# Picked rows in two halves of a PSUM bank, six one-hots under way and a ring of 64 rows: a four-layer graph network on one core

## The chip, the cores and the metric

The kernel runs on one core of a Trainium2 chip. The time is the device time of one execution in microseconds (us), the median of several runs. The engines are TensorE (PE; its weight loads are counted apart as PEld), VectorE (DVE), ScalarE (ACT), GpSimd (POOL) and SyncE (SP). Each engine works through its own list of instructions in order; an instruction that waits holds up everything behind it on that engine.

## The reference, cut to what matters

There are 16 graphs of 1024 nodes with 64 features and a random adjacency of about 16 neighbours a node. Layers 0 and 1 are dense products with the adjacency. Layers 2 and 3 thin out each node's neighbours and aggregate by quantiles: for every node and every feature the values of the node itself and of its remaining neighbours are sorted, and three interpolated quantiles are summed with weights.

```python
# layer 0: tanh(concat(x, adj @ x) @ W1 + b1) @ W2 + b2;   layer 1: (adj / deg) @ x
# layers 2 and 3, each followed by a residual sum and a layer norm:
adj_d = dilate(adj, mask)                # removes every skip-th neighbour, symmetrically
vals  = where((adj_d > 0)[..., None], x[:, None, :, :], big)
sv    = sort(vals, axis=2)               # per node and feature
for tau, wt in zip((0.25, 0.5, 0.75), (0.25, 0.5, 0.25)):
    pos = tau * (m - 1)                  # m: number of values of this node
    agg = agg + wt * (lower + frac * (upper - lower))
y = relu((x + agg) @ W1 + b1) @ W2 + b2
```

## The kernel before

The nodes of a graph are ordered by how many values they have and cut into eight tiles of 128 nodes. Tile t holds up to `SIZES[t]` values a node, and VectorE sorts them with a network of min and max over whole tiles. How a tile's values come into SBUF differs:

- the seven smaller tiles (19, 17, 15, 14, 13, 11 and 10 values, in that order) are gathered by GpSimd from a table in DRAM, one indirect DMA for each value, into a ring of `ROOM` rows. A tile takes adjoining rows of the ring, and its gathers wait until whoever held them has been weighed;
- the largest tile (33 values) is picked by TensorE: for value i VectorE writes a one-hot matrix (`hot`), and 24 matmuls multiply it with the features in three bf16 parts, into PSUM (`pgk`). ScalarE copies the picked rows into `got`.

A "round" k handles layer 2 of graph k together with layer 3 of graph k - 2, so most tiles are sorted as pairs, and there are 18 rounds.

```python
SIZES = (10, 11, 13, 14, 15, 17, 19, 33)
HOTS = 4
ROOM = 72
# ...
def pick(dst, hot, parts, first=True):
    for c in range(NT):
        for q in range(3):
            nc.tensor.matmul(dst, hot[:, c, :], parts[:, c, q, :], start=first and c + q == 0,
                             stop=c == NT - 1 and q == 2)
# ... in fill(k), for the tile of 33 values, for each of the two members:
for g in range(1, size, 8):
    pg = s.psum.tile([P, 8, C], F32, name="pgk", tag="f", bufs=1)      # one PSUM bank
    for i in range(g, g + 8):
        hot = s.lists.tile([P, NT, P], BF, name="hot", bufs=HOTS)
        dve.tensor_scalar(hot, e.place, float(i), None, op0=ALU.is_equal)
        # ... (a first matmul for rows that not all nodes have)
        pick(pg[:, i - g, :], hot, e.parts[m], whole)
        yield 2.1
    yield 2
    nc.scalar.copy(got[:, m, g : g + 8, :], pg)
    yield 0.5
```

The order of every engine's instructions is fixed when the program is built. Each stage is a Python generator; `yield 2.1` says "go on when VectorE has been given 2.1 us more of work", by a rough count of VectorE's work. Between the min and max steps of a sort the kernel lets every generator that is due go on. So `yield` sets a distance in the program, not a wait on the chip.

Three other stages have their distances changed. In `features` (layers 0 and 1):

```python
for h in range(NH):
    pa = s.psum.tile([P, G, C + 1], F32, name="pa", tag="x", bufs=1)
    for q in range(G):
        for jt in range(NT):
            nc.tensor.matmul(pa[:, q, :], adj[i][:, jt, :], x1[:, jt, :], ...)
        yield 4
        # ... near, and the load of the next adjacency block
    yield 6
    dve.tensor_scalar(deg[:, 0], pa[:, :, C], 1.0, None, op0=ALU.max)
```

and earlier in the same stage, two operations on one PSUM tile that the prediction speaks of:

```python
for q in range(G):
    nc.tensor.transpose(px[:C, q * P : (q + 1) * P], x_s[:, h * G + q, :], ident)      # line 427
for q in range(G):
    for jt in range(NT):
        nc.tensor.matmul(px[C:, q * P : (q + 1) * P], x_s[:, jt, :], adj[t][:, jt, :], ...)   # line 431
    if q == 1:
        nc.scalar.copy(node_in[:C], px[:C])                                             # line 434
    yield 5
```

In `lists` (which neighbours remain, and in which order), loops of this form, where TensorE fills one of two PSUM buffers (`pr`, `pv` or `pk`) while ScalarE reads the other:

```python
for t in range(NT + 1):
    if t < NT:
        pr = s.psum.tile([P, N], F32, name="pr", tag="big", bufs=2)
        # ... matmuls into pr
    yield 3
    if t:
        # ... two activations that read prs[t - 1]
    yield 1.2
```

In `ordered`, the stage after it, single products are put at some distance behind what VectorE prepares for them. SBUF is full: a one-hot takes 2 KB of each partition, a row of the ring 512 bytes.

Of the kernel before, what the change touches and what calls it, by code (L numbers as in the profile page):

```python
# [12 lines left out]
F32 = mybir.dt.float32  # L13
F16 = mybir.dt.float16
BF = mybir.dt.bfloat16
# [6 lines left out]
P = 128  # L22
# [4 lines left out]
LEAST = (1,) + SIZES[:-1]  # L27
KS = -(-(max(SIZES[:-1]) - 1) // 8) * 8
KW = max(SIZES)
HOTS = 4  # L30
ROOM = 72
LONG = 40
BIG = 1e30
EPS = 1e-5
# [178 lines left out]
def adj_resnorm_kernel(ctx: ExitStack, tc: tile.TileContext, x, adj_t, nodemask, w01, b01, w02, b02,  # L213
# [189 lines left out]
    def features(b, e):  # L403

        x_s = s.feat.tile([P, NT, C], F32, name="x_s", bufs=1)
        load_x(b, x_s)
        adj = {}

        def load(i):

            if i < 2 * NT:
                adj[i] = s.feat.tile([P, NT, P], F32, name="adj_r", bufs=3)
                cols = slice(i % NT * P, i % NT * P + P)
                nc.sync.dma_start(adj[i], adj_t[entry(b), :, cols].rearrange("o (t p) i -> p (o t) i", p=P))

        load(0)
        load(1)
        x1 = s.feat.tile([P, NT, C + 1], F32, name="x1", bufs=1)
        y = s.work.tile([P, NT, C], F32, name="y_x", bufs=1)
        dve.memset(x1[:, :, C : C + 1], 1.0)  # L420
        yield 8
        for h in range(NH):

            node_in = s.work.tile([P, HALF], F32, name="node_in", bufs=1)
            px = s.psum.tile([P, HALF], F32, name="px", tag="x", bufs=1)
            for q in range(G):
                nc.tensor.transpose(px[:C, q * P : (q + 1) * P], x_s[:, h * G + q, :], ident)
            for q in range(G):
                t = h * G + q
                for jt in range(NT):  # L430
                    nc.tensor.matmul(px[C:, q * P : (q + 1) * P], x_s[:, jt, :], adj[t][:, jt, :], start=jt == 0,  # L431
                                     stop=jt == NT - 1)
                if q == 1:
                    nc.scalar.copy(node_in[:C], px[:C])  # L434
                yield 5
                load(t + 2)
            yield 5
            nc.scalar.copy(node_in[C:], px[C:])
            yield 3
            nc.tensor.matmul(px[:C], w01s, node_in, start=True, stop=True)  # L440
            yield 9
            hid_t = s.work.tile([C, HALF], F32, name="hid_t", tag="node_in", bufs=1)
            nc.scalar.activation(hid_t, px[:C], AF.Tanh, bias=b01c)
            yield 3
            pd = s.psum.tile([P, G, C], F32, name="pd", tag="x", bufs=1)
            for q in range(G):
                nc.tensor.matmul(pd[:, q, :], hid_t[:, q * P : (q + 1) * P], w02s, start=True, stop=False)
                nc.tensor.matmul(pd[:, q, :], ones_row, bias_rows[0], start=False, stop=False)  # L448
                nc.tensor.matmul(pd[:, q, :], ident, x_s[:, h * G + q, :], start=False, stop=True)  # L449
            yield 10  # L450
            nc.scalar.copy(y[:, h * G : (h + 1) * G], pd)
        yield 4
        yield from settle(x1[:, :, :C], y, "x")
        while b and not entries[b - 1].packed:
            yield 2
        near = s.sets.tile([P, NT, N], F16, name="near")
# [3 lines that stand above are left out]
                i = NT + h * G + q  # L460
                t = i - NT
                rows = slice(t * P, (t + 1) * P)
                for jt in range(NT):
                    nc.tensor.matmul(pa[:, q, :], adj[i][:, jt, :], x1[:, jt, :], start=jt == 0, stop=jt == NT - 1)  # L464
# [12 lines left out]
        e.near = near  # L477
        x2 = s.feat.tile([P, NT, C], F32, name="x2", tag="x_s", bufs=1)
        dve.tensor_add(y, y, x1[:, :, :C])
        yield from settle(x2, y, "x")  # L480
        nc.sync.dma_start(table[0][b % 3][:N, :].rearrange("(t p) c -> p t c", p=P), x2)
        while b >= 2 and not entries[b - 2].filled[0]:
            yield 2
        parts = s.feat.tile([P, NT, 3, C], BF, name="x2p")
        yield from split(x2, parts, y)
        e.parts[0] = parts

    def lists(b, e, pace):
# [29 lines left out]
                prs.append(pr)  # L518
                for h in range(NH):
                    cs = range((h + 1) * HALF // P)  # L520
                    for c in cs:
                        nc.tensor.matmul(pr[:, h * HALF : (h + 1) * HALF], near[:, c, t * P : (t + 1) * P],  # L522
                                         steps[:, ONSET + h * HALF - c * P :][:, :HALF], start=c == 0, stop=c == cs[-1])
            yield 3
            if t:
                for i in range(2):
                    junk = s.work.tile([P, N], F16, name="junk", tag="dist", bufs=3)
                    nc.scalar.activation(junk, prs[t - 1], AF.Sign, bias=lim[:, i, t - 1 : t], scale=-1.0,  # L528
                                         accum_out=cut_at[:, i, t - 1 : t])
            yield 1.2  # L530
        yield 5

        mid, off = st[:, 2], st[:, 3]
# [20 lines left out]
        own = s.work.tile([P, NT, 3], F16, name="own", bufs=1)  # L554
        key = s.work.tile([P, 5, NT], F32, name="key_c", bufs=1)
        pvs = []
        for t in range(NT + 1):
            if t < NT:
                rows = slice(t * P, (t + 1) * P)
# [2 lines left out]
                for c in range(NT):  # L562
# [1 line left out]
                    nc.tensor.matmul(pv[:, cols], near[:, c, rows], scaled[:, c, :], start=True, stop=False)  # L564
                    nc.tensor.matmul(pv[:, cols], takes[:, c, rows], minus_n, start=False, stop=False)  # L565
                    nc.tensor.matmul(pv[:, cols], minus_n, takes[:, t, cols], start=False, stop=True)
            yield 2.8
            if t:
                nc.scalar.activation(left(t - 1), pvs[t - 1], AF.Relu)  # L569
# [32 lines left out]
        for t in (*reversed(range(NT)), -1, -2, -3):  # L602
            if t >= 0:
# [30 lines left out]
    def ordered(b, e, order, own):  # L634
# [41 lines left out]
        for g in reversed(range(0, NT, G)):  # L676
# [4 lines left out]
                                     start=c2 == 0, stop=c2 == c)  # L681
            yield 9
            dve.tensor_mul(place[:, g : g + G, :], pp, place[:, g : g + G, :])
        e.place = place

        e.none = s.feat.tile([KW - 1, P], BF, name="none", bufs=5)
        wts = s.feat.tile([P, NT, most_wanted], F32, name="wts", bufs=5)
        for h in range(NH):
# [6 lines left out]
            dve.tensor_scalar(counted, pn[:KW], nth[:KW], None, op0=ALU.is_equal)  # L695
            if h == NH - 1:
                dve.tensor_scalar(e.none, pn[: KW - 1, G - 1, :], nth[: KW - 1], BIG, op0=ALU.is_le, op1=ALU.mult)
            pw = s.psum.tile([P, G, most_wanted], F32, name="pw", tag="s", bufs=1)
            for q in range(G):
                nc.tensor.matmul(pw[:, q, :], counted[:, q, :], weights[:KW, h * G + q, :], start=True, stop=True)  # L700
# [26 lines left out]
    def fill(k):  # L727
# [6 lines left out]
        for m, b, e in members(k):  # L734
            while e.parts[m] is None or e.xs[m] is None or e.place is None or e.none is None:
                yield 1
            nc.scalar.copy(got[:, m, 0, :], e.xs[m][:, t, :])
            for g in range(1, size, 8):
                pg = s.psum.tile([P, 8, C], F32, name="pgk", tag="f", bufs=1)
                for i in range(g, g + 8):  # L740
                    hot = s.lists.tile([P, NT, P], BF, name="hot", bufs=HOTS)
                    dve.tensor_scalar(hot, e.place, float(i), None, op0=ALU.is_equal)
                    whole = i < LEAST[t]
                    if not whole:
                        nc.tensor.matmul(pg[:, i - g, :], e.none,
                                         ident_b[: KW - 1, i - 1 : i].to_broadcast([KW - 1, C]), start=True, stop=False)
                    pick(pg[:, i - g, :], hot, e.parts[m], whole)
                    yield 2.1
                yield 2
                nc.scalar.copy(got[:, m, g : g + 8, :], pg)  # L750
                yield 0.5
            e.filled[m] = True

    def weigh(k, t, got, agg, which):
# [196 lines left out]
    with ExitStack() as main:  # L951
# [309 lines left out]
```

## Time and profile before

| | before |
|---|---|
| time, median of 3 runs | 5402.21 us (5398.02 to 5413.57) |
| span of the profiled execution | 5411.4 us |
| one-hots written by VectorE | 1024, 435 ns each |
| picking matmuls of TensorE | 24576, some 0.2 us each, pipelined |
| copies of picked rows by ScalarE | 128, 584 ns each |
| gathers issued by GpSimd | 2944, 1137 ns each |
| mean granted TensorE clock | 0.753 of full speed |

How to read it: busy time is the time in which an engine executes; the span is shared by all engines. A line of a view of waits says which engine and line waited, for the result of which engine and line, how long in total, how often, and the longest time. A group's line gives its busy time and the mean of one in ns, then the idle time of the engine just ahead of it and what ended it. "issue" is time that no recorded wait explains. The clock is what the throttle granted TensorE, 1.00 being full speed.

### The profile page before, as it was taken

To read this page: it belongs to the slowest core of one execution; us is meant where nothing else is said; L and a number is where in the kernel's file an instruction comes from. 1 tells how busy PE (TensorE), PEld (TensorE's weight loads), DVE (VectorE), ACT (ScalarE), POOL (GpSimd) and SP (SyncE) were. 2 spreads that over 40 slices of the span, in tenths; PEclk is the share of its full clock that TensorE was granted. 3 is DMA by queue.
4 is the path that set the end of the run, shared out by engine and by line. 5 is a ranking of instruction groups with operands and counts; after the bars stand their busy time and mean duration, and the time that the engine had idled before them with its cause. 6 is when DMAs were issued, how large, how long until landed. Compare 5 with 4: busy or idle time off the path is not lost.

```text
span 5411.4 us, 112427 instructions
## 1 busy us (share of the span) xinstructions
PE 3883.9 (72%) x45304; PEld 2975.3 (55%) x45304; DVE 4454.0 (82%) x8819; ACT 2295.4 (42%) x6086; POOL 3677.3 (68%) x3228
## 2 busy tenths in 40 slices
PE   6888877596977959687695968769596876616343
PEld 5656655374755737465573746657374664515332
DVE  2487777989898897878889787887978789979966
ACT  3364453444545363444536344452634445312222
POOL 0335476877777576767768677776867768777562
PEclk7887887696877778686787868678786867756555
DMA  2222222222222211222221122212112211111010
GB/s 82 64 60 55 65 57 50 52 49 59 56 61 48 58 41 45 52 53 59 46 62 42 41 54 56 58 46 58 44 39 58 55 43 23 26 23 26 17 24 10
DMA packets 420187, 259.37 MB, mean 48 GB/s; under 512 B 106165, under 2 KB 368453, under 8 KB 419653
## 3 DMA queue, kind: packets, MB, share of 16 engines
q0 software_dynamic: 102400, 105.06, 10.1%
q1 hardware_dynamic: 317252, 147.02, 9.7%
q8 instruction: 356, 5.83, 0.5%
q14 instruction: 179, 1.46, 0.1%
HBM read 239.27 MB, written 12.58 MB: 47 GB/s over the span
## 4 chain that ended last, share of the span: by engine, by line
DVE 48%; PE 40%; issue 3%; ACT 3%; POOL 3%; DMA 2%; DVEq 0%; POOLq 0%; ACTq 0%
DVE other L207 18%; DVE got_s L207 12%; PE pgk L355 10%; DVE got L207 9%; PE pk L608 8%; PE pa L464 5%; PE px L431 3%; DVE hot L207 2%; POOL got_s L359 2%; DMA got_s<-table,idx 2%; PE ordered_x L355 2%; PE pd L797 1%; PE pd L796 1%; PE pd L449 1%; PE pd L448 1%
## 5 line engine op out<-in xcount | busy, mean ns | idle before, releaser
L359 POOL DMA_INDIRECT got_s<-table,idx x2944 | 3347.8, 1137 | 1487.2 <-issue 662.2
L355 PEld LDWEIGHTS <-hot 128*128 128x128 bf16 x24576 | 949.0, 108 | 595.5 <-DVE hot L207 514.3
L207 DVE TENSOR_SCALAR hot<-place 128x1024 bf16<-128x1024 f16 x1024 | 439.4, 435 | 393.6 <-PE pgk L355 392.8
L355 PE MATMUL pgk<-x3p,hot 128*128 128x64 bf16 x12288 | 563.0, 215 | 251.7 <-DVE hot L207 182.6
L522 PE MATMUL pr<-steps,near 128*128 128x512 bf16 x1536 | 483.5, 486 | 346.1 <-ACT junk L528 190.5
L355 PE MATMUL pgk<-x2p,hot 128*128 128x64 bf16 x12288 | 477.2, 201 | 252.6 <-DVE hot L207 229.3
L762 ACT ACTIVATE got_s<-got_s,wts 128x64 f32<-128x64 f32 x1568 | 399.9, 336 | 384.2 <-DVE got_s L207 383.9
L522 PEld LDWEIGHTS <-near 128*128 128x128 f16 x1536 | 181.2, 119 | 639.0 <-issue 544.9
L207 DVE TENSOR_TENSOR other<-got_s 128x512 f32<-128x512 f32 (+8 forms) x900 | 513.9, 582 | 12.5 <-DMA got_s<-table,idx 0.3
L207 DVE TENSOR_TENSOR got_s<-got_s 128x256 f32<-128x256 f32 (+7 forms) x918 | 491.2, 537 | 19.3
L608 PE MATMUL pk<-near,order 128*128 128x512 f16 x2048 | 478.4, 389 | 0.0
L565 PE MATMUL pv<-minus_n,takes 128*128 128x128 bf16 x1024 | 239.5, 259 | 250.0 <-DVE takes L207 248.9
L207 DVE TENSOR_TENSOR got_s<-other 128x512 f32<-128x512 f32 (+8 forms) x774 | 408.3, 540 | 8.2
L464 PE MATMUL pa<-x,adj_r 128*128 128x65 f32 x2048 | 376.8, 362 | 49.5 <-ACT x L385 26.9
L464 PEld LDWEIGHTS pa<-x,adj_r 128*128 128x128 f32 x2048 | 361.4, 275 | 74.4 <-ACT x L385 27.2
L565 PEld LDWEIGHTS <-takes 128*128 128x128 bf16 x1024 | 118.3, 116 | 422.7 <-DVE takes L207 278.5
L564 PE MATMUL pv<-scaled,near 128*128 128x128 f16 x1024 | 240.9, 260 | 138.1 <-ACT near L569 137.8
L207 DVE TENSOR_TENSOR other<-other 128x128 f32<-128x128 f32 (+13 forms) x558 | 319.1, 572 | 14.8
L608 PEld LDWEIGHTS <-order 128*128 128x128 bf16 x2048 | 196.4, 100 | 230.8 <-issue 24.6
L750 ACT COPY got<-pgk 128x512 f32<-128x512 f32 x128 | 74.7, 584 | 546.6 <-PE pgk L355 546.6
L528 ACT ACTIVATE junk<-pr,nb_st 128x1024 f16<-128x1024 f32 x256 | 282.1, 1108 | 31.6 <-PE pr L522 30.3
L431 PE MATMUL px<-adj_r,x_s 128*64 128x128 f32 x2048 | 263.3, 285 | 8.8 <-ACT node_in L434 7.4
(204 smaller groups left out, 7532.0 us busy)
## 6 DMA issues: line engine op xcount, KB each, us to landing
adj_r<-in_adj_dram SPq DMA_DIRECT2D x256, 512.0 KB
got_s<-table,idx POOLq DMA_INDIRECT x2944
x_s<-in_x_dram SPq DMA_DIRECT2D x16, 256.0 KB
table<-x SPq DMA_DIRECT2D x16, 256.0 KB
x<-table SPq DMA_DIRECT2D x16, 256.0 KB
table<-x3s,rows POOLq DMA_INDIRECT x128
out_dram<-agg,out_rows POOLq DMA_INDIRECT x128
table<-no_row SPq DMA_DIRECT2D x6, 0.2 KB
```

Of the source, the lines that this page charges most:

```text
L207: return call(*args, **kwargs)
L355: nc.tensor.matmul(dst, hot[:, c, :], parts[:, c, q, :], start=first and c + q == 0, stop=c == NT - 1 and q == 2)
L359: nc.gpsimd.indirect_dma_start(out=dst, out_offset=None, in_=tab, in_offset=bass.IndirectOffsetOnAxis(ap=rows, axis=0))
L431: nc.tensor.matmul(px[C:, q * P : (q + 1) * P], x_s[:, jt, :], adj[t][:, jt, :], start=jt == 0, stop=jt == NT - 1)
L464: nc.tensor.matmul(pa[:, q, :], adj[i][:, jt, :], x1[:, jt, :], start=jt == 0, stop=jt == NT - 1)
L522: nc.tensor.matmul(pr[:, h * HALF : (h + 1) * HALF], near[:, c, t * P : (t + 1) * P], steps[:, ONSET + h * HALF - c * P :][:, :HALF], star ...
L528: nc.scalar.activation(junk, prs[t - 1], AF.Sign, bias=lim[:, i, t - 1 : t], scale=-1.0, accum_out=cut_at[:, i, t - 1 : t])
L564: nc.tensor.matmul(pv[:, cols], near[:, c, rows], scaled[:, c, :], start=True, stop=False)
L565: nc.tensor.matmul(pv[:, cols], takes[:, c, rows], minus_n, start=False, stop=False)
L608: nc.tensor.matmul(cols, order[:, c, t * P : (t + 1) * P], left(c, slice(h * G, (h + 1) * G)), start=c == 0, stop=c == NT - 1)
L750: nc.scalar.copy(got[:, m, g : g + 8, :], pg)
L762: nc.scalar.activation(prods[:, m, i, :], got[:, m, slot_id, :], AF.Copy, scale=e.wts[:, t, i : i + 1])
```

## The change

The change has four parts.

1. Up to six one-hots may be under way in place of four. The 4 KB that this takes of each partition comes from the ring, which shrinks from 72 to 64 rows.
2. The picked rows go to two halves of one PSUM bank in turn, four rows each. The copy of a half is placed after the second pick into the other half, so that TensorE need not stop between two groups.
3. In the loops of `lists` the distance between ScalarE's reading and TensorE's next matmuls into the same buffer grows (1.2 to 3, 1 to 2.6, 1.5 to 3), and the distance between TensorE's matmuls and the reading shrinks by as much.
4. A few products are placed later: 3 us before the first `pv`, 8 in place of 6 before `deg`, and 3 us more at two places of `ordered`.

```diff
-HOTS = 4
-ROOM = 72
+HOTS = 6
+ROOM = 64
@@ features, before deg
-            yield 6
+            yield 8
@@ lists, loop of pr
-            yield 3
+            yield 1.2
             if t:
                 # ... two activations that read prs[t - 1]
-            yield 1.2
+            yield 3
@@ lists, before and in the loop of pv
+        yield 3
         for t in range(NT + 1):
             # ... matmuls into pv
-            yield 2.8
+            yield 1.2
             if t:
                 # ... two activations, the first reads pvs[t - 1]
-            yield 1
-        yield 4
+            yield 2.6
+        yield 3
@@ lists, loop of pk
-            yield 4
+            yield 2.5
             # ... copy of pks[done]
-            yield 1.5
+            yield 3
@@ ordered, after place and after counted
+            yield 3
@@ fill
-            for g in range(1, size, 8):
-                pg = s.psum.tile([P, 8, C], F32, name="pgk", tag="f", bufs=1)
-                for i in range(g, g + 8):
-                    # ... hot and pick
-                    yield 2.1
-                yield 2
-                nc.scalar.copy(got[:, m, g : g + 8, :], pg)
-                yield 0.5
+            waiting = None
+            def empty():
+                nc.scalar.copy(got[:, m, waiting[0] : waiting[0] + 4, :], waiting[1])
+            for i in range(1, size):
+                if i % 4 == 1:
+                    first, pg = i, pgs[i // 4 % 2]
+                # ... hot and pick, into pg[:, i - first, :]
+                yield 2.1
+                if i % 4 == 2 and waiting:
+                    empty()
+                if i % 4 == 0:
+                    waiting = first, pg
+            yield 5
+            empty()
+            yield 0.5
@@ before the rounds
+        picked = s.psum.tile([P, 8, C], F32, name="pgk", bufs=1)
+        pgs = [picked[:, :4, :], picked[:, 4:, :]]
```

More of the change, by code (lines that the diff above doesn't have):

```diff
@@ L697, in ordered @@
                 dve.tensor_scalar(e.none, pn[: KW - 1, G - 1, :], nth[: KW - 1], BIG, op0=ALU.is_le, op1=ALU.mult)
+            yield 3
             pw = s.psum.tile([P, G, most_wanted], F32, name="pw", tag="s", bufs=1)
@@ L737, in fill @@
             nc.scalar.copy(got[:, m, 0, :], e.xs[m][:, t, :])
-            for g in range(1, size, 8):
-                pg = s.psum.tile([P, 8, C], F32, name="pgk", tag="f", bufs=1)
-                for i in range(g, g + 8):
[L741 to L747, printed above, removed]
-                    yield 2.1
-                yield 2
-                nc.scalar.copy(got[:, m, g : g + 8, :], pg)
-                yield 0.5
+            waiting = None
[4 more added lines that the diff above has]
+                    first, pg = i, pgs[i // 4 % 2]
+                hot = s.lists.tile([P, NT, P], BF, name="hot", bufs=HOTS)
+                dve.tensor_scalar(hot, e.place, float(i), None, op0=ALU.is_equal)
+                whole = i < LEAST[t]
+                if not whole:
+                    nc.tensor.matmul(pg[:, i - first, :], e.none,
+                                     ident_b[: KW - 1, i - 1 : i].to_broadcast([KW - 1, C]), start=True, stop=False)
+                pick(pg[:, i - first, :], hot, e.parts[m], whole)
+                yield 2.1
[6 more added lines that the diff above has]
+            yield 0.5
             e.filled[m] = True
```

## The prediction, made before the changed kernel was run

> **What bounds the kernel now.** I began with the page's busy times, to see whether one engine is full.
>
> ```profile
> span 5411.4 us, 112427 instructions
> PE 3883.9 (72%) x45304; PEld 2975.3 (55%) x45304; DVE 4454.0 (82%) x8819; ACT 2295.4 (42%) x6086; POOL 3677.3 (68%) x3228
> ```
>
> None is, but VectorE is nearest: 4454.0 us is a floor that the change leaves alone, and 957 us of the span are VectorE's idle time. So the second view is what VectorE waited for, over the whole span:
>
> ```profile
> DVE hot L207 <- PE pgk L355: 392.8, 169, 7.3
> DVE deg L207 <- PE pa L464: 88.6, 20, 6.2
> ```
>
> 393 of the 957 us are VectorE about to write a one-hot while TensorE still reads the one that stood in that buffer four earlier. To see where, I took one round of the steady part. In the chain in order of time the same piece ("DVE other", 4.50 us) returns at 2570.11, 2887.32 and 3204.92, so a round lasts 317 us. Here it is cut into stretches (TensorE, weight loads, VectorE, ScalarE and GpSimd busy; then granted clock, DMA share, GB/s):
>
> ```profile
> 2887.00:2957.00 70.00, 31.85 (x268) 24.27 (x267) 68.50 (x96) 47.29 (x96) 56.92 (x43) 0.72 0.17 43
> 2957.00:2997.00 40.00, 36.48 (x451) 30.22 (x452) 38.42 (x89) 18.58 (x46) 31.77 (x28) 0.72 0.19 37
> 2997.00:3057.00 60.00, 59.26 (x849) 41.77 (x848) 35.63 (x63) 17.09 (x37) 41.35 (x43) 1.00 0.26 60
> 3057.00:3107.00 50.00, 42.61 (x638) 36.45 (x636) 46.58 (x92) 18.24 (x60) 22.14 (x16) 0.79 0.08 17
> 3107.00:3137.00 30.00, 30.00 (x296) 27.36 (x295) 18.50 (x43) 6.56 (x26) 23.30 (x23) 0.50 0.37 95
> 3137.00:3205.00 68.00, 44.03 (x340) 25.87 (x336) 65.38 (x132) 35.44 (x118) 53.37 (x49) 0.75 0.26 62
> ```
>
> Two stretches hold the loss. In 2997 to 3057 TensorE is full (59.26 of 60) and VectorE works 35.63; in 3107 to 3137 TensorE is full and VectorE works 18.50. Elsewhere VectorE is all but full while TensorE idles. So the bound changes inside the round: VectorE, then TensorE, and the four one-hot buffers are all that lets one run ahead of the other. The third view is what TensorE waited for in four rounds (2570 to 3840 us):
>
> ```profile
> PE pv L565 <- DVE takes L207: 71.5, 24, 12.1
> PE pr L522 <- ACT junk L528: 60.4, 12, 8.1
> PE pv L564 <- ACT near L569: 50.2, 16, 9.1
> ...
> PE pgk L355 <- DVE hot L207: 36.3, 26, 4.8
> PE pgk L355 <- ACT got L750: 12.1, 7, 2.7
> ```
>
> The reader should check where these fall: the pr and pv work lies at 2887 to 2950 and 3165 to 3205, where VectorE does not wait for TensorE at all. The fourth view is GpSimd in the same four rounds:
>
> ```profile
> L359 POOL DMA_INDIRECT got_s<-table,idx x737 | 845.0, 1147 | 306.6 <-issue 170.3 <-DVE other L207 81.0 <-DMA got_s<-table,idx 28.3
> L808 POOL DMA_INDIRECT table<-x3s,rows x32 | 46.5, 1453 | 24.0 <-ACT x3s L385 15.5 <-issue 7.0 <-ACT got_s L762 1.2
> L808 POOL DMA_INDIRECT out_dram<-agg,out_rows x32 | 39.1, 1222 | 9.7 <-issue 4.0 <-ACT got L762 3.0 <-DMA got_s<-table,idx 1.5
> ```
>
> A gather costs 1.147 us and about 0.30 us of issue after it. 737 x 1.447 = 1066 us, and the 64 scatters with their gaps some 105 us: 1171 of 1270 us, 92%, or 293 us of each 317 us round. GpSimd looks 68% busy on the page and is in truth the second bound, with about 24 us of slack a round, most of it the 81.0 us of waiting for ring rows.
>
> **What the Trainium skill says.** "TensorE: Matmul & The Clock Gate", part 1 (the HAM clock gate): after an idle window of about 3.4 us TensorE runs at half rate, and sustained work lifts that; the practical advice is to leave no such gaps. The trace agrees only in part: 3107 to 3137 is 30 us of full TensorE at a granted clock of 0.50. Filling gaps is therefore no promise of a faster clock, and I count none. The same page, part 2 (what happens when you issue a matmul), says matmuls stay in program order; the trace agrees, a pv that waits 12.1 us for takes holds everything behind it. "PSUM — Partial Sum Buffer", on bank collisions, says two engines must not touch one bank and the same 32 partitions at once, whatever the columns, and that software must keep them apart. If this program does that by bank, two halves of one bank are no double buffer. The trace has a test, the copy of px into node_in at line 434, whose data the transposes of line 427 wrote:
>
> ```profile
> L427 PE MATMUL px<-ident,x_s x8: 272/349/418, 2940.5 to 3003.6; 128*64 128x128 f32 x8
> ...
> L434 ACT COPY node_in<-px x2: 579/579/579, 2949.9 to 3013.6; 64x512 f32<-64x512 f32 x2
> ...
>   PE px L431: 9.2, 2
> ```
>
> The transposes were over by 3004, the copy began at 3013.6, and ScalarE had stood idle for the matmuls of line 431, which write other partitions of the bank. So waits here go by bank, and I expect the same for the halves.
>
> **The change part by part.**
>
> *Six one-hots.* VectorE may lead by two more. In 2997 to 3057 it made 13 one-hots in 35.63 us of its own work, one per 2.74 us, so two more are worth up to 5.5 us; in 3107 to 3137 nine in 18.50 us, 2.06 us each, up to 4.1 us. That caps the gain at 9.6 of the 31 us that a round loses (125.0 us in four). A longer lead makes the deg wait longer (6.1 us a round, it needs TensorE to have caught up), so I take 6.5 us. Laying the recorded TensorE and VectorE durations end to end with six buffers in place of four gave 6.2 us a round. Over 13 rounds: -85 us.
>
> *TensorE's parts behind what they wait for.* pr waits 60.4/4 = 15.1 us and pv 50.2/4 = 12.6 us a round for ScalarE. With ScalarE placed 3.0 (was 1.2) and 2.6 (was 1.0) ahead of the next matmuls, against two activations of 1.1 to 1.3 us, nearly all of that should go. But it lies where VectorE is full: worth nothing in a steady round, and some 20 us in all in the first rounds, where VectorE idles with it. deg placed 8 instead of 6 after pa: 2 us a round at best, partly eaten by the longer lead; -15 us over the span.
>
> *Two halves.* Copies go from 128 of 584 ns to 256 of about 372 ns (the 128x256 copy of line 451 has that mean): 95 us for 75, on an engine with room. By bank, the third pick of a group waits for the copy of the other half, and that for the second pick: twice as many round trips, and none of the half microsecond that stood behind each copy. Now they cost TensorE 12.1/4 = 3.0 us a round; doubled and shortened by the smaller copy 4.8. So +1.8 us where TensorE is the bound, +25 us over 14 rounds.
>
> *A ring of 64 rows.* Tiles come as 19, 17, 15, 14, 13, 11, 10. 72 rows hold the first four (65), 64 hold three (51). Placing them by hand, a tile now needs the tile four or five before it to be freed; with 64, three, at times four. The timelines give the lead (a tile's sort ends where its first weight begins on ScalarE): in steady rounds gathers end about 100 us before the sort (the 13's ended at 2999.8, its sort began about 3107), and one tile of lead is 24 to 80 us, so most rounds can pay. At the ends they can't: in the last full round the leads of the 13, 11 and 10 are 34, 23 and 14 us, and in the third round the 10's was 49. I charge 20 us there and 40 us over the last four rounds: +60 us.
>
> Sum: -85 - 20 - 15 + 25 + 60 = -35 us, and 5402 - 35 is about 5367.
>
> **The rivals.** (a) GpSimd becomes the bound. For it: 92% full, and a lost tile of lead cannot be made up. Against: waiting VectorE lets TensorE catch up, so the two waits do not add. If each steady round lost 6 us more, the gain would be eaten: about 5450. (b) The halves really are independent, TensorE never waits for a copy, and ScalarE, no longer held, runs weights earlier; then the +25 turns into some -30 and the time is near 5300. The px lines speak against it. (c) The distances straighten TensorE so far that its clock stays up: the clocks of 0.72, 0.79 and 0.50 say that some 73 us of 2957 to 3137 ran at half rate, and a third of them regained would be 10 us a round, 5240. Against it the 30 us at 0.50 with no gap.
>
> **Range and chances.** The ring (20 to 120) and the one-hots (50 to 120) are each uncertain by some 50 us, the rest by 40; together near 90 either way: 5270 to 5470. Faster by over 2% means below 5294, which needs a rival to be right; slower by over 2%, above 5510, needs the ring to bind in every round. 0.2, 0.7, 0.1.
>
> **What would show it.** Right: hot's wait for pgk falls from 393 to about 300 us and is still VectorE's longest; the pr and pv waits for ScalarE fall below a third while the steady round shortens by only 5 to 8 us; TensorE's wait for got doubles from 65 us; VectorE waits for gathers in the third round and the last ones; GpSimd waits longer for ring rows. Wrong: a steady round under 303 us (rival c or b), or gathers heading VectorE's waits in the middle of the span (rival a).

## The result, and the profile after

The changed kernel takes 5379.86 us (median of 4 runs, 5377.75 to 5385.83); the kernel before, run beside it, 5407.51 us. The ratio is 0.9952, with a 95% interval of 0.9933 to 0.9972: a gain of 28 us, or half a per cent. Predicted were 5367 us and a range of 5270 to 5470.

The page of the changed kernel begins:

```profile
span 5376.9 us, 112554 instructions
PE 3746.3 (70%) x45268; PEld 2875.6 (53%) x45304; DVE 4444.1 (83%) x8819; ACT 2296.3 (43%) x6214; POOL 3659.3 (68%) x3228
```

VectorE and ScalarE are as busy as before (4454.0 and 2295.4 us). So the gain has to be looked for in what VectorE waited for. The view of VectorE's waits, changed kernel (waiting engine and line, what it waited for, total us, times, longest us):

```profile
DVE hot L207 <- PE pgk L355: 127.2, 58, 6.9
DVE y_m L207 <- ACT y_m L812: 115.7, 13, 20.3
DVE other L207 <- DMA got_s<-table,idx: 75.5, 10, 19.2
DVE place L207 <- PE pp L681: 75.3, 15, 9.3
DVE near L207 <- DMA adj_r<-in_adj_dram: 65.5, 14, 9.9
```

The one-hot's wait fell from 392.8 to 127.2 us, a fall of 266 us, and deg's, further down in this view, from 88.6 to 19.0. The kernel gained 28. What came in place are the next four lines. VectorE's wait for y_m, which it takes from ScalarE, was this before:

```profile
DVE y_m L207 <- ACT y_m L800: 33.7, 2, 20.3
```

Its wait for gathers (DMA got_s) was 0.3 us before, for place 21.8, for near 17.0.

The same shift shows in ScalarE's own waits. The copy of picked rows waited for picks, first in the kernel before, then in the changed one:

```profile
ACT got L750 <- PE pgk L355: 546.6, 96, 11.3
```

```profile
ACT got L744 <- PE pgk L355: 1175.5, 196, 18.6
```

ScalarE stands twice as long before these copies. Their own work is as predicted, 256 of 369 ns or 94.5 us, in place of 128 of 584 ns or 75 us; the idle time ahead of them was not.

Of TensorE's waits in the changed kernel, those for ScalarE of which the prediction speaks (three longer ones, for hot, takes and nb_st, are left out):

```profile
PE pr L522 <- ACT junk L528: 149.4, 46, 8.8
PE pv L565 <- ACT near L570: 93.8, 30, 7.3
PE pgk L753 <- ACT got L744: 56.2, 81, 3.4
PE pgk L355 <- ACT got L744: 45.5, 48, 3.7
```

pr and pv waited 190.5 and 137.8 us for ScalarE before, so they lost a fifth and a third, not the two thirds hoped for. The wait for the copy went from 69.0 us (65.2 + 3.8) to 101.7.

Last, the crowded part of a steady round of the changed kernel, up to the end of the tile of 33 (two of its stretches; columns as in the prediction: TensorE, weight loads, VectorE, ScalarE, GpSimd, then clock, DMA share, GB/s):

```profile
2982.00:3042.00 60.00, 53.38 (x803) 38.84 (x800) 43.17 (x77) 21.80 (x63) 27.00 (x29) 0.91 0.09 17
3042.00:3082.00 40.00, 31.70 (x465) 27.96 (x464) 30.62 (x68) 8.18 (x33) 31.24 (x26) 0.84 0.28 69
```

Before, TensorE was full in two stretches of the crowded part (59.26 of 60, 30.00 of 30) and busy 42.61 of the 50 us between them. From 2982 to 3082 neither it (85.08 of 100) nor VectorE (73.79 of 100) is full: here they wait for each other and for ScalarE, the idlest of the three (29.98 of 100).

### The profile page after: what moved, and what is told of

It reads as the page before. It is cut to its first block, busy times and chain, and to the rows that moved or that the text cites. A ratio compares the mean times of both kernels' runs of the same rounds, so it can differ in the third digit from the quotient of the medians.

```text
span 5376.9 us, 112554 instructions
## 1 busy us (share of the span) xinstructions
PE 3746.3 (70%) x45268; PEld 2875.6 (53%) x45304; DVE 4444.1 (83%) x8819; ACT 2296.3 (43%) x6214; POOL 3659.3 (68%) x3228
## 5 line engine op out<-in xcount | busy, mean ns | idle before, releaser
L355 PEld LDWEIGHTS <-hot 128*128 128x128 bf16 x24576 | 881.8, 104 | 611.8 <-DVE hot L207 468.2
L522 PE MATMUL pr<-steps,near 128*128 128x512 bf16 x1500 | 435.1, 453 | 378.0 <-ACT nb_st L503 223.8
L355 PE MATMUL pgk<-x3p,hot 128*128 128x64 bf16 x12288 | 493.2, 204 | 229.0 <-DVE hot L207 203.0
L355 PE MATMUL pgk<-x2p,hot 128*128 128x64 bf16 x12288 | 478.6, 201 | 239.1 <-DVE hot L207 216.1
L744 ACT COPY got<-pgk 128x256 f32<-128x256 f32 x256 | 94.5, 369 | 1186.0 <-PE pgk L355 1175.5
L207 DVE TENSOR_SCALAR hot<-place 128x1024 bf16<-128x1024 f16 x1024 | 436.5, 437 | 129.8 <-PE pgk L355 127.2
L207 DVE TENSOR_TENSOR got_s<-got_s 128x384 f32<-128x384 f32 (+7 forms) x918 | 490.7, 537 | 17.5
L464 PE MATMUL pa<-x,adj_r 128*128 128x65 f32 x2048 | 355.2, 349 | 93.4 <-DMA adj_r<-in_adj_dram 39.2
L566 PE MATMUL pv<-minus_n,takes 128*128 128x128 bf16 x1024 | 224.7, 249 | 279.0 <-DVE takes L207 278.4
L464 PEld LDWEIGHTS pa<-x,adj_r 128*128 128x128 f32 x2048 | 343.4, 264 | 107.6 <-DMA adj_r<-in_adj_dram 40.5
L565 PE MATMUL pv<-scaled,near 128*128 128x128 f16 x1024 | 226.2, 250 | 105.0 <-ACT near L570 93.8
L431 PE MATMUL px<-adj_r,x_s 128*64 128x128 f32 x2048 | 274.7, 293 | 2.1 <-ACT node_in L434 1.4
```

What stands on the lines that cost most here:

```text
L207: return call(*args, **kwargs)
L744: nc.scalar.copy(got[:, m, waiting[0] : waiting[0] + 4, :], waiting[1])
```

## The experiments

**How the runs are read.** Besides medians I use three readings of the traces. The first is the time at which the tile of 33 has been sorted (its first weight starts on ScalarE) in rounds 2, 6 and 13; the difference of the last two, divided by 7, is the length of a steady round. The second adds up the lines of VectorE's waits by the engine they wait for. The third is the granted clock in the stretch from the first to the last pick of a round, as a mean of the seven such stretches between the ends of rounds 6 and 13.

| kernel | median us | ends of rounds 2 / 6 / 13 | steady round | VectorE waits for TensorE / ScalarE / DMA | ScalarE waits for picks | clock in the picks |
|---|---|---|---|---|---|---|
| before | 5402 | 1047 / 2294 / 4517 | 317.5 | 505 / 234 / 71 | 555 | 0.81 |
| one-hots and ring (one_hots_look) | 5352 | 1063 / 2277 / 4418 | 305.9 | 242 / 390 / 127 | 553 | 0.86 |
| and distances (no_halves) | 5314 | 1027 / 2241 / 4416 | 310.7 | 305 / 311 / 123 | 601 | 0.82 |
| one-hots, ring and halves (one_hots_halves) | 5475 | 1080 / 2333 / 4546 | 316.0 | 225 / 508 / 125 | 1098 | 0.85 |
| changed: all parts | 5380 | 1027 / 2240 / 4464 | 317.7 | 238 / 388 / 161 | 1176 | 0.86 |
| changed, quarters | 5297 | 1041 / 2247 / 4379 | 304.6 | 133 / 450 / 106 | 885 | 0.90 |
| quarters, two banks | 5246 | 1036 / 2241 / 4325 | 297.8 | 157 / 380 / 104 | 656 | 0.94 |

All columns but the median are from one profiled execution each; the one of no_halves took 5332 us, the longest of its four. "Waits for picks" counts all matmuls of line 355, of which up to 12.0 us are another product.

**1. Each part alone: one_hots_alone, ring_64_alone, halves_alone, distances_alone.** The kernel before with one part of the change each:

```diff
# one_hots_alone                 # ring_64_alone
-HOTS = 4                        
+HOTS = 6                        
-ROOM = 72                       -ROOM = 72
+ROOM = 64                       +ROOM = 64
# halves_alone: the hunks "fill" and "before the rounds" of the change
# distances_alone: the hunks "features", "lists" and "ordered" of the change
```

> The kernel before with six one-hots and a ring of 64 rows, nothing else changed. The prediction's terms for these two are -85 and +60 us, so 5402 - 25 = about 5380. Theory C (the copies of halves hold ScalarE, and that eats the gain of the one-hots): without the halves VectorE's waits for y_m and best stay near 0, ScalarE's wait for picks stays at 550 to 700 us, a steady round takes 311 us or less, and the time is at or below 5350. Theory L (a longer lead only moves the wait to the next thing that stands behind TensorE's list): hot's wait falls from 393 to about 130 us, but waits for place, deg, y_m or best rise by nearly as much, a steady round stays at 315 to 318 us, and the time is 5385 to 5430 with the ring's cost.

> The kernel before with a ring of 64 rows and nothing else. The prediction's term: +60 us (20 to 120), 20 of it in the third round and 40 in the last four, steady rounds unchanged. If GpSimd's lead was mere surplus (rival): within 10 us of before, with VectorE's wait for gathers below 20 us in all. If GpSimd becomes the bound everywhere (rival): steady rounds over 320 us, above 5450.

> The kernel before with the two halves of the bank and the copy two slots later, four one-hots, ring of 72, old distances. The prediction's term: +25 us from twice as many round trips; TensorE's wait for got doubles from 69 us. Theory C: ScalarE's wait for picks rises from 547 us to 900 or more, and a steady round gets longer, 319 to 322 us; time 5410 to 5450. Rival (the shorter fill helps where filling is on the path, in the first two rounds): the first tile of 33 ends some 15 to 19 us earlier and the time is 10 to 20 us below before.

> The kernel before with the changed distances of features, lists and ordered alone. The prediction's terms: -20 in the first rounds and -15 for deg, about 5370. Theory L: a steady round stays at 317 us within 1, while TensorE's waits for junk and near fall; time within 20 us of before. Rival (the added 3 us at four places lengthen the way to place and its one-hots): place waited for by VectorE rises above 50 us, time above 5420.

These four landed on a chip where the kernel before took 7309 us in place of 5402, so they can be compared only with each other. TensorE's waits of one_hots_alone show why:

```profile
PE pgk L355 <- issue: 993.5, 1175, 35.1
```

TensorE stood still before picks 1175 times, some 0.85 us each, and no recorded wait explains it. Against the kernel before on that chip the ratios are 0.9954 [0.9938, 0.9971] for one-hots and ring, 0.9927 [0.9906, 0.9949] for the ring alone, 0.9968 [0.9952, 0.9985] for the halves and 1.0123 [1.0098, 1.0148] for the distances. They tell nothing of the 5402 us: in one_hots_alone VectorE is busy 61% of the span and GpSimd 48%, in place of 82% and 68%. The next kernels ask the same questions with several parts at once, where the kernel before takes 5405 to 5411 us.

**2. One-hots and ring again: one_hots_look.** The same two lines as in one_hots_alone.

> The kernel before with six one-hots and a ring of 64 rows, once more; in the runs of the parts alone TensorE stood still for some 1000 us in front of picks with nothing recorded that it waited for, and the kernel before took 7309 us beside them in place of 5402, so their waits do not speak of the change. Where the kernel before takes 5402 again: the prediction's terms are -85 and +60, about 5380. Theory C (the copies of halves hold ScalarE and eat the gain of the one-hots): ScalarE's wait for picks 550 to 700 us, y_m and best waits near 0, a steady round of 311 us or less, 5350 or below. Theory L (the longer lead only moves the wait): hot's wait about 130 us, others up by nearly as much, a steady round of 315 to 318 us, 5385 to 5430.

Measured: 5351.55 us against 5410.78, ratio 0.9897 [0.9877, 0.9916], 59 us faster. VectorE's waits, one_hots_look:

```profile
DVE best L207 <- ACT code L619: 132.1, 47, 6.6
DVE hot L207 <- PE pgk L355: 110.6, 46, 9.7
DVE other L207 <- DMA got_s<-table,idx: 97.8, 11, 20.3
```

The one-hot's wait fell by 282 us. A steady round lost 11.6 us (317.5 to 305.9), more than the 9.6 that the prediction held to be the most. deg, at 76.0 us over the span, did not grow. Time and steady round are as theory C expected; that best would not be waited for (132.1 us) is not, there theory L was right. The gathers' 97.8 us lie at the two ends: 21.4 us between 900 and 1100, 73.9 after 4450, and 0.2 us in the four steady rounds from 2558 to 3827. By the ends of rounds, the kernel was 16 us *behind* at round 2, caught up 33 by round 6 and 81 more by round 13 (114 together), and gave back 34 us after that (spans of 5347.0 and 5411.4 us, so 928.8 us after round 13 in place of 894.7). So the ring's price is at least some 16 + 34 = 50 us.

Is it the longer lead that shortened the steady round? The clock says that it is only part of it. Here are stretches from first to last pick, with the same number of matmuls each: one of the kernel before, then two of one_hots_look (columns as above):

```profile
2957.31:3146.41 189.10, 177.76 (x2379) 144.64 (x2379) 147.85 (x306) 60.95 (x169) 125.82 (x114) 0.81 0.22 51
```

```profile
2912.70:3090.64 177.94, 168.20 (x2379) 136.15 (x2379) 147.93 (x307) 60.73 (x169) 132.43 (x120) 0.86 0.23 55
3520.73:3707.53 186.80, 177.06 (x2379) 144.56 (x2379) 148.08 (x307) 60.73 (x169) 138.24 (x127) 0.81 0.21 54
```

TensorE is busy 94 to 95% of each, and length times clock is 153.2, 153.0 and 151.3 us (151 to 155 in all seven of one_hots_look): TensorE sets the length of this stretch, with four one-hots as with six. In the third stretch the clock stayed as before, and the round around it took 314.5 us, 3.0 less than before; the six others took 302.5 to 308.3 us, at clocks of 0.84 to 0.88. In that one round VectorE waited 8.3 us for one-hot buffers in place of some 31, but 11.2 us for deg in place of 6.1. So at an equal clock six one-hots gave 3.0 us of the 11.6; the rest came together with a higher clock. The kernel before shows the other side: its round that ended at 1659.5 us took 306.8 us with four one-hots, at a clock of 0.87 in the picks. That is one round of each kernel, and no run holds the clock fixed; why it rose is open.

**3. The change without its halves: no_halves.** The changed kernel with the old filling:

```diff
-            for i in range(1, size):
-                if i % 4 == 1:
-                    first, pg = i, pgs[i // 4 % 2]
+            for g in range(1, size, 8):
+                pg = s.psum.tile([P, 8, C], F32, name="pgk", tag="f", bufs=1)
+                for i in range(g, g + 8):
                 # ... hot and pick
+                yield 2
+                nc.scalar.copy(got[:, m, g : g + 8, :], pg)
```

> The changed kernel with the filling of before: six one-hots, ring of 64, the new distances, but eight picked rows to a copy and no halves. One-hots and ring alone gave 5352 us and a steady round of 306 us, the whole change 5380 and 317. Theory C (copies of halves, which wait by bank, hold ScalarE): without them ScalarE's wait for picks falls from 1176 back to some 550 us and the steady round to 305 to 309 us, time 5330 to 5360. Theory D (the new distances put place, adjacency loads and the like too late for the round): steady round stays at 315 to 319, VectorE's waits for place and near stay, time 5375 to 5400.

Measured: 5314.42 us against 5405.18, ratio 0.9823 [0.9807, 0.9839]. So the halves, which were to keep TensorE from stopping, cost the change 65 us (5314 to 5380; ratios 0.9823 and 0.9952). VectorE's waits for TensorE did not rise with them (305 without, 238 with); those for ScalarE rose from 311 to 388, and those for DMA from 123 to 161. One line rises by more than the whole loss, that for y_m, of which 115.7 us were seen in the changed kernel. In no_halves:

```profile
DVE y_m L207 <- ACT y_m L803: 38.4, 5, 20.4
```

Against it counted fell by 37 us and place by 19, while near rose by 25. The clock does not explain the loss: in the picks it is higher with halves (0.86) than without (0.82). Neither theory fits whole. The time is below C's 5330 to 5360 and the steady round, 310.7 us, above its 309; place and near are still waited for (33.8 and 13.6 us in four rounds), as D said.

Against one_hots_look the run also gives the distances: 37 us faster (5352 to 5314). By the ends they bring 36 us by round 2 and nothing from there to round 6. From 6 to 13 they lose 34, and at the end they gain 14 again (914.8 us after round 13 against 928.8). These profiled runs differ by only 17 us, not 37, as that of no_halves was its slowest. In the four steady rounds VectorE waits 33.8 us for place here, against 10.2 in one_hots_look, and 2.4 for deg against 17.1. The clock in the picks is also lower, 0.82 against 0.86; which of the two costs the 34 us is not shown. Over the whole span the wait that fell most is that for best, from the 132.1 us above; it is VectorE's wait for ScalarE's copy `code` in the pk loop, where the distance between the two went from 1.5 to 3. In no_halves:

```profile
DVE best L207 <- ACT code L620: 40.6, 31, 4.1
```

**4. Halves with one-hots, without distances: one_hots_halves.** The edit of section 2, and the hunks "fill" and "before the rounds" of the change.

> Six one-hots, ring of 64 and the halves, with the distances of before. Theory C: ScalarE's wait for picks about 1150 us, VectorE waits for y_m, best and place behind it, steady round 315 to 319 us, time 5375 to 5400. Theory D: steady round 305 to 309 us, time 5330 to 5360, ScalarE's long waits cost nothing.

Measured: 5475.33 us against 5405.18, ratio 1.0135 [1.0113, 1.0157]: 124 us slower than the same kernel without halves, and 75 us above what theory C expected at most. VectorE's waits for TensorE are no longer than without them (225 against 242), those for ScalarE rose by 118 us, from 390 to 508, and ScalarE's own wait for picks doubled. First one_hots_look, then one_hots_halves:

```profile
ACT got L750 <- PE pgk L355: 544.2, 95, 19.1
```

```profile
ACT got L741 <- PE pgk L355: 1095.6, 206, 16.8
```

And y_m again, in the same order:

```profile
DVE y_m L207 <- ACT y_m L800: 33.3, 3, 18.4
```

```profile
DVE y_m L207 <- ACT y_m L809: 113.1, 14, 20.3
```

The loss, then, is not the round trip of TensorE but ScalarE, which is held. How, the timelines of the changed kernel show. ScalarE (start, duration, line and operation; in brackets the idle time before it and what ended it):

```profile
2993.30 0.37 ACT L744 COPY got<-pgk 128x256 f32<-128x256 f32 x1 [12.25 <-PE pgk L355]
2993.57 1.02 ACT L620 CAST code<-pk 128x1024 f16<-128x1024 f32 x1
2994.47 0.94 ACT L812 ACTIVATE y_m<-pd,mask_s 128x64 f32<-128x64 f32 x4
```

TensorE in the same stretch, and below it VectorE:

```profile
2981.37 0.87 PE L355 MATMUL pgk<-x2p,hot 128*128 128x64 bf16 x24
...
2990.05 0.87 PE L355 MATMUL pgk<-x2p,hot 128*128 128x64 bf16 x24
...
2992.39 0.87 PE L355 MATMUL pgk<-x2p,hot 128*128 128x64 bf16 x24
2993.72 0.18 PE L753 MATMUL pgk<-ident_b,none 32*128 32x64 bf16 x1 [0.46 <-ACT got L744]
```

```profile
2995.44 0.69 DVE L207 TENSOR_TENSOR y_m<-y_m,x2s 128x512 f32<-128x512 f32 x1 [7.04 <-ACT y_m L812]
```

The four rows to be copied were complete at 2982.24. The copy waited until 2993.26, the end of the second pick into the *other* half. Behind it in ScalarE's list stood y_m, whose product pd was ready at 2985.03 (TensorE's L809, left out above); it was read at 2994.47, and VectorE stood 7.04 us for it. TensorE itself lost 0.46 us to the copy. Such a copy is placed two picks late so that its rows are surely there. As the wait goes by the bank, it waits for both later picks too, with everything behind it. ("By the bank" stands for: not by the rows that are read. The two halves are slices of one tile that fills one bank, and no run tells whether tile or bank decides.)

**5. A control and two real banks: quarters, two_banks.** No PSUM bank was free. The last stage of a round (a product with W1, a relu, a product with W2, the mask: PSUM tiles pt, ph, pd) used one bank for 512 columns at a time. In `quarters` it goes over 256 columns at a time, at half the distances, in half of its bank:

```diff
-        for h in range(NH):
-            pt = s.psum.tile([P, HALF], F32, name="pt", tag="m", bufs=1)
+        W = HALF // 2
+        for h in range(2 * NH):
+            pt = fin[0]
             # ... the same steps over half the columns, ph and pd in fin[0] too
-            yield 7
+            yield 3.5
@@ before the rounds
+        shared = s.psum.tile([P, HALF], F32, name="fin", bufs=1)
+        fin.append(shared[:, : HALF // 2])
```

`two_banks` is `quarters` with the second half of the picked rows in the part of that bank which has come free:

```diff
-        pgs = [picked[:, :4, :], picked[:, 4:, :]]
+        pgs = [picked[:, :4, :], shared[:, HALF // 2 :].rearrange("p (i c) -> p i c", c=C)]
```

> Control for the next: the changed kernel, with the last product chain (pt, ph, pd of finish) worked in four quarters of 256 columns in half of its bank instead of two of 512, at half the distances; the picked halves still share one bank. Both theories: within 25 us of the changed kernel's 5380, ScalarE's wait for picks about 1150 us.

> As the control, but the second half of the picked rows lies in the unused half of the bank of finish, so that the two halves are in two banks. Theory C: a copy waits for its own half's last pick alone, ScalarE's wait for picks falls below 700 us, TensorE's wait for got (102 us in the changed kernel) below 40, VectorE's waits for y_m and best fall, and the time is 40 us or more below the control. Theory D: ScalarE's wait falls too, but the steady round stays within 3 us of the control's and the time within 20.

Measured: quarters 5296.84 us, ratio 0.9794 [0.9776, 0.9813]; two_banks 5246.02 us, 0.9703 [0.9686, 0.9719]. Both stood against 5405.18. The first is outside the 25 us around 5380 that both theories allowed; of the second every number that theory C expected came true. Between the two the only difference is the bank (and, with it, the tile), and it is worth 51 us. TensorE's wait for got went from 104.2 us in quarters (61.4 + 42.8) to 17.9. ScalarE's waits before the copy, quarters, then two_banks (the second half bears the name of the shared tile, fin):

```profile
ACT got L744 <- PE pgk L355: 884.1, 189, 13.5
```

```profile
ACT got L744 <- PE pgk L355: 171.8, 47, 10.1
```

With 103.1 and 56.2 us for the last stage's products (L796; L809 and L801) and 81.2 for picks into fin (L355), the copy waits 412 us in place of 884 in the control. Part of that has only moved: since the last stage now shares a bank with picks, its own activations wait for them (h_t 140.5, o_t 139.6, y_m 121.3 us). Over all, ScalarE waits 656 us for picks against 885 in the control, and VectorE waits 380 us for ScalarE against 450. Those 70 us less for ScalarE, 24 more for TensorE and 2 less for DMA make 48, which agrees with the 51 gained. Of single lines best fell by 37 us, y_m only from 109.5 to 97.5: the banks are not free of each other even here. The clock in the picks rose as well, from 0.90 to 0.94; how much of the 51 us goes through it was not separated.

That the control itself gained 83 us was not expected. In its four steady rounds place and near are no longer waited for, and the one-hot's wait is 21.3 us (45.5 in the change); the clock in the picks is 0.90 in place of 0.86. Which of its three differences does that (shorter pieces, half the distances, other places of all that follows) was not isolated.

two_banks is the fastest kernel of the study, 159 us under the kernel before it was run beside.

**6. Ring alone again, the old filling with quarters, and another split: ring_64_look, quarters_eights, two_banks_5_68.**

```diff
# ring_64_look: ring_64_alone again
# quarters_eights: quarters, filled in groups of eight as in no_halves
# two_banks_5_68: two_banks with
-HOTS = 6
-ROOM = 64
+HOTS = 5
+ROOM = 68
```

> The kernel before with a ring of 64 rows alone, on a chip on which TensorE does not stand still without a recorded reason. The prediction's term: +60 us (20 to 120). One-hots and ring together gave -54, so with the term right the one-hots alone would be worth -114, above the prediction's cap of -125 for 13 rounds at 9.6 us. Rival (the lead was mere surplus): 0 to 15 us, and the one-hots are worth -55 to -70. VectorE's wait for gathers, 0.3 us before: 80 to 100 us in both cases, since it was 98 with one-hots and ring.

> The control with quarters (5297 us), with eight picked rows to a copy and no halves, in a bank of their own. Theory C: the halves in one bank cost here too, as they did with the old finish (65 us), so 5230 to 5270, like the two banks' 5246 or better. Rival (in quarters the halves cost nothing, and two banks gain by halves that are really apart): 5285 to 5305. ScalarE's wait for picks 500 to 600 us.

> The two banks' version (5246 us) with five one-hots and a ring of 68 rows, which holds the four largest gathered tiles again. If the ring's cost is what is left (VectorE's wait for gathers of 77 us falls below 30): 5190 to 5230. If the sixth one-hot is worth as much: 5235 to 5260.

These came to lie on a chip of the first kind again (before 7256.06 us; in ring_64_look TensorE stands 893.7 us at "issue" before picks). Ratios there: 0.9901 [0.9862, 0.9940], 0.9709 [0.9673, 0.9744] and 0.9848 [0.9813, 0.9884]. The ring alone, the halves on top of quarters, and the split 5 and 68 are therefore not measured for the ordinary case. That a smaller ring is faster on such a chip, twice, has no explanation here.

## Why the prediction came out right in sum, and where its steps failed

The sum was -35 us and the result -28. That the two are so near is luck: one-hots and ring together gave 34 us more than predicted, the halves cost 40 more.

| step | predicted | measured | from |
|---|---|---|---|
| six one-hots and ring together | -25 | -59 | one_hots_look against the kernel before |
| of it six one-hots | -85 | -114, read off | ends of rounds 2 to 13, one_hots_look |
| of it ring of 64 rows | +60 | +50, read off | round 2, and after round 13, one_hots_look |
| distances | -35 | -37 | one_hots_look to no_halves |
| two halves | +25 | +65 | no_halves to the changed kernel |

The runs of the first row and the last two lead step by step from the kernel before to the changed one, so that their sum, -31, must come near -28; it is no check. The split of the first row is read off one trace, whose span differs by 64 us.

*The bound.* Right. VectorE's work is unchanged, and what moved the time is its waits. In the four steady rounds from 2558 to 3827 it waited 150 us for TensorE and 2 for ScalarE before; in the changed kernel 79 for TensorE, 47 for ScalarE and 23 for DMA. 152 became 149, and the steady round stayed as it was (317.5 and 317.7). The step "the steady round shortens by only 5 to 8 us" is therefore wrong as a whole: it was 11.6 us shorter with one-hots and ring, and the distances (4.8) and the halves (7.0) took that back. The gain lies elsewhere: 21 us by the end of round 2 and 34 from there to round 6, none from 6 to 13, and 19 lost again after that.

*One-hots.* That the wait for one-hot buffers would shrink was right; what it is worth was not. A round became 11.6 us shorter, not 6.5. The step that failed is "Filling gaps is therefore no promise of a faster clock, and I count none". TensorE sets the length of the stretch of picks, and there the granted clock was 0.86 on average in place of 0.81 (section 2). In the one round where it stayed at 0.81, 3.0 us were gained, which is less than the 6.5; and there deg's wait grew from 6.1 to 11.2 us, as the prediction had it. So it is the clock, which the prediction had set to nothing, by which the cap of 9.6 was passed, as far as one such round can tell. In four steady rounds there were 49 waits for one-hot buffers (125.0 us) before and 12 (30.9 us) in one_hots_look: 23.5 us of waits a round, of which at an equal clock 3.0 us were time. In the changed kernel hot's wait fell to 127 us, not 300, and is still the longest, but barely (115.7 for y_m).

*Ring.* Right in place and, as far as it can be read, in size: nothing in the steady rounds, waits for gathers in the third round and the last four. GpSimd's waits for ring rows (for other, got_s and the weights that ScalarE puts into got_s) rose only from 319 to 342 us, so "GpSimd waits longer for ring rows" holds, weakly. The ring without the one-hots was not measured in the ordinary case; the 50 us are read from their joint run.

*Distances.* The total is right and the reason in part. The gain lies in the first rounds, as predicted, but is 36 us there; VectorE's waits that fell in them are those for gathers (23.7 to 5.1 us), best (33.3 to 20.5) and deg (30.8 to 19.5). The waits of pr and pv fell to 149 and 94 us and not "below a third": in no_halves, where ScalarE is not held by halves, they are 135 and 90. The largest fall, 91.5 us for best, is of a wait that the prediction does not name. deg fell from 76.0 us to 26.8 there; against both, place rose (54.0 to 94.7 us), counted (1.6 to 53.6) and near (13.7 to 41.0). So -35 was reached by another way than the one given. With halves present the same distances are worth 95 us (5475 to 5380): what a distance is worth depends on the other parts.

*Halves.* This step failed. The deduction that waits do not go by rows but by bank was right: it is what "PSUM — Partial Sum Buffer" of the Trainium skill led to (bank collisions: two engines may not touch one bank and the same 32 partitions, whatever the columns), the copy that waited 12.25 us for a pick into the other half agrees, and two_banks shows the price. But I charged it to TensorE's round trips, doubled to 4.8 us a round (how 3.0 doubled comes to 4.8 the working does not show). They grew only by half, by 33 us in all (69.0 to 101.7), and VectorE's waits for TensorE fell. The words that failed are "on an engine with room". ScalarE is 43% busy and has no room in the sense needed: it works in order, and a copy that waits up to 18.6 us holds y_m, which VectorE wants next. In the two comparisons without and with halves, VectorE's wait for y_m rose by 77 and 80 us (38.4 to 115.7, 33.3 to 113.1) and the time by 65 and 124. In the second deg (45 us) and rows (31) rose too; why these did is not shown.

*The rivals.* (b), independent halves, is out for the change as built, but the independence itself, measured from quarters, is worth 51 us, near the 55 us that lay between +25 and -30. (a) was not seen: gathers head no wait in the middle of the span. (c) was seen in part: over the span the mean clock went only from 0.753 to 0.765, but in the picks from 0.81 to 0.86. It was not the distances that did it, with them the clock in the picks fell from 0.86 to 0.82; and the changed kernel's steady round did not get below 303 us.

Open: what sets the clock in the picks, and how much of each part's worth goes through it; why finishing in quarters is worth 83 us; what the ring and the two more one-hots are worth each alone; and what stops TensorE on the chips of section 1.

## What to carry to other kernels

An engine that is idle more than half of the time has no room if it works in order: ask of each instruction put on it how long it may wait, and who needs what stands behind it. Two halves of a PSUM bank are no double buffer where waits go by bank; a reader placed late "to be safe" then waits for the very work it was to lie beside. And a wait for an engine that is full is not worth its length: more buffers took 23.5 us of such waits out of a round, and where the clock stayed the same the round was 3.0 us shorter. Compare such stretches at the same granted clock before the gain is put down to the buffers.

## What the runs showed of the hardware that was not expected

On two of the chips TensorE stands still for 0.7 to 0.9 us before picks, 993 to 1222 times in a run, with no recorded cause, and the kernel before takes 7256 and 7309 us in place of 5402. And a full TensorE is not always a fast one: before, it was 30.00 of 30.00 us busy at a granted clock of 0.50, and 59.26 of 60 at 1.00, while in the changed kernel a stretch with gaps (53.38 of 60) had 0.91. The same 2379 matmuls of a round's picks took 189.1 us at a clock of 0.81 and 177.9 us at 0.86.
